# Four state sums at a time in TensorE's column groups, and the D and skip terms as diagonal matmuls, in a selective-scan stage

## The chip, the cores and the metric

The kernel runs on one NeuronCore of a Trainium2 chip. The metric is the device time of one execution in microseconds (us); the median over several runs is compared. The engines are TensorE (PE in the profile; PEld is its weight load), VectorE (DVE), ScalarE (ACT), GpSimd (POOL) and the DMA-issuing SyncE (SP). Each takes its instructions in the order in which the program issues them, and engines wait for each other by semaphores.

## The reference

The program is a convolution, state-space and attention hybrid, followed by an attention layer and a routed mixture of experts, on x of shape (4, 256, 32, 32). The part that matters here is the state-space block. The 256 channels are split in NB = 4 groups of 64; each group of each of the 4 images passes through:

```python
def selective_scan(u, dt, Bm, Cm, A, Dp):
    dA = jnp.exp(dt[..., None] * A)
    dBu = (dt * u)[..., None] * Bm[:, :, None, :]
    def step(h, inp):
        dA_t, dBu_t, C_t = inp
        h = dA_t * h + dBu_t
        return (h, jnp.einsum('bds,bs->bd', h, C_t))
    ...
    return ys.transpose(1, 0, 2) + u * Dp
...
    y = selective_scan(u, dt, Bm, Cm, -jnp.exp(alog), dp)
    return y * jax.nn.silu(z) @ outw.T
...
xm = mamba_v(xc, ...) + skip_scale * xc
```

There are 128 inner channels d, 16 states s and 1024 time steps. So each of the 16 pairs of group and image needs 128 x 16 recurrences over 1024 steps, then the sum over states of h times C, the term u * D, the gate silu(z), the output projection, and the skip term.

## The kernel before, in words

A tile of 128 partitions holds 8 channels times 16 states, with time along the free dimension. So a pair (the profile's blocks of 16 steps, n = 0 to 15) takes 16 tiles, j = 0 to 15, and the stage has 256 steps t = 16 n + j. The main loop of the stage (L808 to L837) is written out by hand, and nothing reorders it. In step t it issues:

- on VectorE, dBu times B (L813), in place in PSUM, then the scan (L816), which writes the tile hs;
- on GpSimd, hs times C (L817);
- on VectorE and GpSimd, when j = 2, `gated` of the pair before: u times D plus pY (L479), then times the gate sz (L480);
- on TensorE, `select(t + 2)` (L770): two bf16 matmuls that spread the rows of dt * u that belong to tile t + 2 over the states. Its PSUM tile dBu has two buffers, so it waits for scan t;
- on TensorE, `add_up(t - 2)` (L778): two fp32 matmuls of 128x128 by 128x512 that add hs over the states into pY. The weight is a window in a 0/1 strip that puts the 8 sums on the 8 right rows of pY and zeros elsewhere, accumulated over the 16 tiles;
- on SP, `fetch(t + 4)` (L758), the broadcast load of dt for a tile (dA, five buffers), and on ScalarE `decay(t + 3)` (L763), the exponential of it;
- the steps of `front` for the next pair (L388 to L464): four projections at j = 11 to 14 (L400), Silu at 15, then the dt projection at 0 (L411), ScalarE functions at 1, `rest` at 3 (L422, VectorE), `log` at 4 (L425, and on GpSimd L426), `dt_out` at 5 (L429), `times_u` at 6 (L434), the bf16 parts at 8 and 10 (L438 to L444), `spread` of B and C at 8 and 9 (L457, L459), and the transfers of `turn` at 11 (L449, L452);
- for the pair before, `project_out` at j = 6 (L487) and, on VectorE, `store` at j = 7 (L493): the skip scale times xm plus the projection, in place; and at j = 10 `gate` of the present pair (L472, L474).

All the large projections share one PSUM tile, mm. The tile hs comes from the pool `scan` with four buffers; the scan of step t overwrites the hs of step t - 4, which L778 must have read.

```python
hs = hss[t] = sp.tile([P, N], F32, tag="hs", name="hs")
nc.vector.tensor_tensor_scan(hs, dAs.pop(t), dBu, 0.0, ALU.mult, ALU.add)
nc.gpsimd.tensor_tensor(hs, hs, r["C"], ALU.mult)
if j == 2 and n > 0:
    gated(n - 1)
select(t + 2)
add_up(t - 2)
fetch(t + 4)
decay(t + 3)
```

Ahead of this loop a short planned stage normalises x and makes the first pair's inputs; the images' x tiles lie in the hs buffers (two images) and in the pool `lnA`. Behind it come the convolutions, two attentions and the experts, which the diff doesn't touch.

Of the kernel before, what the change touches and what calls it, by code (L numbers as in the profile page):

```python
# [10 lines left out]
F32 = mybir.dt.float32  # L11
BF16 = mybir.dt.bfloat16
AF = mybir.ActivationFunctionType
ALU = mybir.AluOpType
# [4 lines left out]
N = HH * WW  # L19
NP = N + 2  # L20
P = 128
# [295 lines left out]
def body(tc, g, out):  # L317
# [5 lines left out]
    def pool(name, bufs, **kw):  # L323
        return tc.tile_pool(name=name, bufs=bufs, **kw)

    with pool("const", 1) as cp, pool("dram", 1, space=bass.MemoryType.DRAM) as drp, contextlib.ExitStack() as late:
# [16 lines left out]
        def V(name, j=0, n=1):  # L343
            return vec[:, VOFF[name] + j : VOFF[name] + j + n]
# [28 lines left out]
        with pool("mconst", 1) as mc, pool("front", 1) as fp, pool("dts", 2, space=bass.MemoryType.DRAM) as dsp, pool(  # L373
# [5 lines left out]
            aneg = mc.tile([P, NB * DS], F32, tag="aneg", name="aneg")  # L379

            def block(nb, b):
                q0 = (nb % 2) * DM
                return slice(q0, q0 + DM), XM[b][q0 : q0 + DM, nb // 2]
# [4 lines left out]
            def front(n):  # L388
# [32 lines left out]
                def rest():  # L421
                    stt(r["e"], r["pdt"], -1.0, r["e"], ALU.add, ALU.subtract)  # L422

                def log():
                    act(r["pdt"], r["pdt"], AF.Ln)  # L425
                    nc.gpsimd.tensor_tensor(r["dt"], r["dt"], r["e"], ALU.subtract)  # L426

# [48 lines left out]
            def gated(n):  # L476
                nb, b = order[n]
                u = state[n]["u"]
                stt(u, u, V("dd", nb), state[n]["pY"], ALU.mult, ALU.add)  # L479
                nc.gpsimd.tensor_tensor(u, u, state[n]["sz"], ALU.mult)  # L480

            def project_out(n):
                nb, b = order[n]
                rows_out, xb = block(nb, b)
                po = state[n]["po"] = big()
                for h in HALVES:
                    mm(po[rows_out, h], m_out[:, nb, :], state[n]["u"][:, h], start=True, stop=True)  # L487

            def store(n):
                nb, b = order[n]  # L490
                rows_out, xb = block(nb, b)
                xb = xb[:, XL : XL + N]
                stt(xb, xb, V("skip")[rows_out], state[n]["po"][rows_out], ALU.mult, ALU.add)  # L493

            state = {}
            with pool("scan", 4) as sp, pool("yps", 1, space=PSUM) as yps, pool("dps", 2, space=PSUM) as dps, pool("lnA", 1) as wp:

# [7 lines left out]
                add, pre.spare, pre.slack, pre.split = pre.add, (2, 3), 700, True  # L505
                xs = [[sp.tile([P, N], F32, tag="hs", name="hs") for k in range(CT)] for b in range(2)]
                for b in range(2, B):
                    t = wp.tile([P, CT, N], F32, tag=f"xs{b}", name=f"xs{b}")
                    xs.append([t[:, k] for k in range(CT)])
# [8 lines left out]
                m_dt = load("m_dt", [DTR, NB, DIN], where=mc)  # L518
                pickf = wp.tile([96, 32 // DB, P], F32, tag="pickf", name="pickf")
                nc.sync.dma_start(out=pickf, in_=g["pick"].rearrange("k (j p) -> k j p", j=32 // DB))  # L520
# [157 lines left out]
                def weights():  # L678
# [74 lines left out]
                dAs, dBus, hss = {}, {}, {}  # L753

                def fetch(t):
                    if t < NBLK:
                        dAs[t] = sp.tile([P, N], F32, tag="dA", name="dA", bufs=5)
                        nc.sync.dma_start(out=dAs[t], in_=state[t // NJ]["ds"][t % NJ].unsqueeze(0).to_broadcast([DS, DB, N]))  # L758

                def decay(t):  # L760
                    if t < NBLK:
                        c = order[t // NJ][0] * NJ + t % NJ
                        act(dAs[t], dAs[t], AF.Exp, scale=aneg[:, c : c + 1])  # L763

                def select(t):
                    if t < NBLK:
                        j = t % NJ
                        dBus[t] = dps.tile([P, N], F32, tag="dBu", name="dBu")
                        for h in HALVES:
                            mm(dBus[t][:, h], pick[:, j % 4], state[t // NJ]["U"][:, j // 4, h], start=True, stop=True)  # L770

                def add_up(t):
                    if 0 <= t < NBLK:
                        r, j, hs = state[t // NJ], t % NJ, hss.pop(t)
                        if j == 0:
                            r["pY"] = yps.tile([P, N], F32, tag="y", name="pY")
                        for h in HALVES:
                            mm(r["pY"][:, h], strip[:, P - DB - j * DB : 2 * P - DB - j * DB], hs[:, h], start=j == 0, stop=j == NJ - 1)  # L778

# [1087 lines left out]
```

## Time and profile before

| what | us |
| --- | --- |
| time, median of 3 runs (lowest, highest) | 3326.42 (3322.93, 3326.98) |
| the profiled execution's own time | 3332.46 |
| its span, first to last instruction | 3330.7 |
| stage of the scans, first L813 to last scan's end | 103.06 to 1197.82 = 1094.8 |
| busy in that stage: VectorE, TensorE, GpSimd, ScalarE | 958.0, 890.5, 775.5, 573.9 |
| granted TensorE clock in that stage, share of full | 0.93 |

A line of the timeline gives the start, the busy time, the engine, the source line, the operation, output and inputs, the shapes, and in brackets the idle time before it with the instruction whose end released it. Matmul ends are modelled; starts are better than ends for telling how long TensorE was occupied. A group line of the page gives the total busy time, the mean ns of one, then the idle time before such instructions and what ended most of it.

### The profile page before, as it was taken

Reading aid. Unit: us, or ns where it says so; the run is one execution under the profiler, and the core shown is the slowest. Engines: PE = TensorE matmul, PEld = TensorE weight load, DVE = VectorE, ACT = ScalarE, POOL = GpSimd, SP = SyncE. Lnnn points to the kernel's source line nnn. Section 1 sums busy time; section 2 is a strip of 40 time slices with the busy share of each in tenths; the row PEclk is TensorE's granted clock in tenths of the full one; section 3 lists DMA queues with packets and bytes.
Section 4 is the critical chain, followed back from the end, with each engine's and each line's share of the span. In section 5 each row is a group of like instructions: output and inputs, shape, how many; then the busy total and the mean of one; then the engine's idle time right before and its main releaser. Section 6 shows DMA issues by size and latency. Waiting matters only on the chain. (4 is left out here: it accounts for less than half of the span.)

```text
span 3330.7 us, 38748 instructions
## 1 busy us (share of the span) xinstructions
PE 2907.4 (87%) x15274; PEld 1693.4 (51%) x15274; DVE 2077.2 (62%) x2347; ACT 1513.0 (45%) x2086; POOL 1223.0 (37%) x763
## 2 busy tenths in 40 slices
PE   7787788878888668998889989989899999899997
PEld 4333333333333224555555554655555656689996
DVE  5789888888888954746496478557364445511112
ACT  3646445554455423545673574565443333311111
POOL 0677767667767730000000010000002222556662
PEclk7899999998999988999999989999999999999998
DMA  3566555656557630000000000000000000465455
GB/s 125 133 159 160 152 145 149 167 145 156 143 150 170 153 113 0 1 1 1 26 1 1 26 1 1 1 14 1 1 13 7 13 7 14 117 193 131 117 124 157
DMA packets 92872, 265.50 MB, mean 80 GB/s; under 512 B 18182, under 2 KB 36086, under 8 KB 89360
## 3 DMA queue, kind: packets, MB, share of 16 engines
q1 hardware_dynamic: 64000, 198.46, 22.7%
q0 software_dynamic: 26512, 60.35, 7.1%
q10 hardware_dynamic: 2176, 4.19, 0.3%
q8 instruction: 121, 1.98, 0.2%
q14 instruction: 63, 0.52, 0.1%
HBM read 291.70 MB, written 42.80 MB: 100 GB/s over the span
## 5 line engine op out<-in xcount | busy, mean ns | idle before, releaser
L817 POOL TENSOR_TENSOR hs<-hs,bc 128x1024 f32<-128x1024 f32 x256 | 602.1, 2357 | 277.1 <-DVE hs L816 276.9
L816 DVE TENSOR_TENSOR_SCAN hs<-dA,dBu 128x1024 f32<-128x1024 f32 x256 | 585.4, 2287 | 73.8 <-PE pY L778 44.0
L778 PE MATMUL pY<-hs,const 128*128 128x512 f32 x1024 | 530.1, 643 | 15.6 <-DVE u L479 12.8
L763 ACT ACTIVATE dA<-dA,aneg 128x1024 f32<-128x1024 f32 x256 | 287.4, 1144 | 331.6 <-DMA dA<-ds 331.1
L1082 DVE TENSOR_REDUCE nm<-s 128x1 f32<-128x1024 f32 x256 | 301.6, 1219 | 203.4 <-PE s L1077 202.7
L1087 ACT ACTIVATE pr<-s,nm 128x1024 f32<-128x1024 f32 x256 | 284.9, 1116 | 196.9 <-DVE nm L1082 194.7
L1101 PE MATMUL k<-const,pr 128*128 128x128 f32 x2048 | 301.1, 291 | 72.8 <-ACT pr L1087 49.1
L1172 POOL TENSOR_TENSOR b<-b,misc 128x1024 f32<-128x1024 f32 x16 | 36.4, 2299 | 893.3 <-DVE misc L1168 835.0
L1101 PEld LDWEIGHTS k<-const,pr 128*128 128x128 f32 x2048 | 234.1, 147 | 191.8 <-issue 82.4
L770 PE MATMUL dBu<-U,pick 96*128 96x512 bf16 x512 | 162.7, 401 | 186.3 <-DVE hs L816 182.4
L813 DVE TENSOR_TENSOR dBu<-dBu,bc 128x1024 f32<-128x1024 f32 x256 | 311.8, 1218 | 4.0 <-PE dBu L770 3.9
L778 PEld LDWEIGHTS pY<-hs,const 128*128 128x128 f32 x1024 | 208.4, 205 | 204.4 <-issue 165.6
L1077 PE MATMUL s<-b,b 32*128 32x512 f32 x1024 | 286.9, 648 | 3.3 <-ACT pr L1087 3.3
L1107 ACT COPY pT<-k 128x512 f32<-128x512 f32 x320 | 175.8, 593 | 173.0 <-PE k L1101 171.8
L1742 PE MATMUL s<-pT,b 128*128 128x128 f32 x1920 | 230.0, 276 | 3.4 <-DMA b<-we,intse 2.9
L1742 PEld LDWEIGHTS s<-pT,b 128*128 128x128 f32 x1920 | 226.1, 192 | 8.6 <-ACT pT L1745 4.0
L770 PEld LDWEIGHTS <-pick 96*128 96x128 bf16 x512 | 41.8, 99 | 370.3 <-issue 303.6
L1107 DVE COPY pT<-k 128x512 f32<-128x512 f32 x192 | 131.6, 686 | 99.7 <-PE k L1101 85.4
L1746 DVE TENSOR_TENSOR pT<-pT,s 128x512 f32<-128x512 f32 x72 | 49.4, 687 | 228.2 <-ACT pT L1745 228.1
L1121 PE MATMUL k<-pT,b 128*32 128x128 f32 x4096 | 152.2, 290 | 17.9 <-DVE pT L1107 14.8
L1121 PEld LDWEIGHTS k<-pT,b 128*32 128x32 f32 x4096 | 113.1, 115 | 74.4 <-issue 31.1
L1077 PEld LDWEIGHTS s<-b,b 32*128 32x128 f32 x1024 | 102.4, 190 | 91.8 <-issue 76.5
(434 smaller groups left out, 4430.4 us busy)
## 6 DMA issues: line engine op xcount, KB each, us to landing
dA<-ds SPq DMA_DIRECT2D x256, 512.0 KB, 4.8
dq<-parts SPq DMA_DIRECT2D x15, 768.0 KB, 3.3
U<-dq SPq DMA_DIRECT2D x45, 256.0 KB, 4.1
ds<-dt SPq DMA_DIRECT2D x16, 512.0 KB, 3.0
b<-x SPq DMA_DIRECT2D x4, 1024.0 KB, 7.2
acc<-pr SPq DMA_DIRECT2D x8, 512.0 KB, 5.8
xm<-x SPq DMA_DIRECT2D x4, 1024.0 KB, 5.0
tokens<-pr SPq DMA_DIRECT2D x8, 512.0 KB, 2.9
```

What stands on the lines that cost most here:

```text
L763: act(dAs[t], dAs[t], AF.Exp, scale=aneg[:, c : c + 1])
L778: mm(r["pY"][:, h], strip[:, P - DB - j * DB : 2 * P - DB - j * DB], hs[:, h], start=j == 0, stop=j == NJ - 1)
L813: tt(dBu, dBu, r["B"], ALU.mult)
L816: nc.vector.tensor_tensor_scan(hs, dAs.pop(t), dBu, 0.0, ALU.mult, ALU.add)
L817: nc.gpsimd.tensor_tensor(hs, hs, r["C"], ALU.mult)
L1077: mm(S[i][:, HALVES[h]], qT[rr, qt * P : (qt + 1) * P], kT[rr, HALVES[h]], start=True, stop=True)
L1082: "DVE", 1220, lambda i=i, u=u: nc.vector.tensor_reduce(nms[u], S[i], AX.X, ALU.max, negate=True),
L1087: "ACT", 1330, lambda i=i, u=u, hd=hd: act(prs[u % 4], S[i], AF.Exp, bias=nms[u], scale=1.0, accum_out=rss[b % 2][:, k, qt, hd : hd + 1]), ...
L1101: nc.tensor.transpose(bank.t[:, j * P : (j + 1) * P], prs[u][:, c0 : c0 + P], ident)
L1107: lambda dst=dst, bank=bank, on_act=on_act: (nc.scalar.copy if on_act else nc.vector.tensor_copy)(dst, bank.t),
L1121: mm(bank.t[i * HD : (i + 1) * HD, 0:P], v[:, 4 * jh + j, hd * HD : (hd + 1) * HD], pTs[m][jh][:, i, j * P : (j + 1) * P], start=j == 0, s ...
L1742: mm(p12[:, a, c], wbufs[w][:, o : o + P], xT[:, k], start=k == 0, stop=k == CT - 1)
```

## The change

- `add_up` does nothing in three steps of four. In the fourth it adds four hs tiles at once: eight fp32 matmuls with 32-column weights, tile i to rows 32 i to 32 i + 31 of pY, for each half of the columns. To make this fit, step t now takes tile `which(t)` of its pair (0, 4, 8, 12, 1, 5, ...), in `fetch`, `decay` and `select` alike.
- With the second group of a pair, two full matmuls with diag(D) add u * D into pY. `gated` becomes one VectorE product of pY and sz; its GpSimd product is gone.
- `project_out` first multiplies xm by diag(skip) into the same PSUM rows, two more matmuls; `store` becomes a copy on ScalarE.
- The GpSimd subtraction of `log` (j = 4) moves to `rest` (j = 3).
- The pool `scan` gets six buffers for hs; the x tiles of a third image move into them, and pickf into the sz tile. Five diagonal matrices are made at the start.

```diff
+            ddiag = mc.tile([P, NB, P], F32, tag="ddiag", name="ddiag")
+            sdiag = mc.tile([P, P], F32, tag="sdiag", name="sdiag")
...
                 def rest():
                     stt(r["e"], r["pdt"], -1.0, r["e"], ALU.add, ALU.subtract)
+                    nc.gpsimd.tensor_tensor(r["dt"], r["dt"], r["e"], ALU.subtract)
 
                 def log():
                     act(r["pdt"], r["pdt"], AF.Ln)
-                    nc.gpsimd.tensor_tensor(r["dt"], r["dt"], r["e"], ALU.subtract)
...
             def gated(n):
-                nb, b = order[n]
-                u = state[n]["u"]
-                stt(u, u, V("dd", nb), state[n]["pY"], ALU.mult, ALU.add)
-                nc.gpsimd.tensor_tensor(u, u, state[n]["sz"], ALU.mult)
+                tt(state[n]["u"], state[n]["pY"], state[n]["sz"], ALU.mult)
...
                 for h in HALVES:
-                    mm(po[rows_out, h], m_out[:, nb, :], state[n]["u"][:, h], start=True, stop=True)
+                    mm(po[rows_out, h], sdiag[rows_out, rows_out], xb[:, XL + h.start : XL + h.stop], start=True, stop=False)
+                    mm(po[rows_out, h], m_out[:, nb, :], state[n]["u"][:, h], start=False, stop=True)
...
-                xb = xb[:, XL : XL + N]
-                stt(xb, xb, V("skip")[rows_out], state[n]["po"][rows_out], ALU.mult, ALU.add)
+                nc.scalar.copy(xb[:, XL : XL + N], state[n]["po"][rows_out])
...
-            with pool("scan", 4) as sp, ...
+            with pool("scan", 6) as sp, ...
...
-                xs = [[sp.tile([P, N], F32, tag="hs", name="hs") for k in range(CT)] for b in range(2)]
-                for b in range(2, B):
+                xs = [[sp.tile([P, N], F32, tag="hs", name="hs") for k in range(CT)] for b in range(B - 1)]
+                for b in range(B - 1, B):
...
+                    for nb in range(NB):
+                        add("DVE", 150, lambda nb=nb: ts(ddiag[:, nb], ident, V("dd", nb), None, ALU.mult))
+                    add("DVE", 150, lambda: ts(sdiag, ident, V("skip"), None, ALU.mult))
...
+                def which(t):
+                    return t % 4 * 4 + t % NJ // 4
...
                 def add_up(t):
-                    if 0 <= t < NBLK:
-                        r, j, hs = state[t // NJ], t % NJ, hss.pop(t)
-                        if j == 0:
+                    if 0 <= t < NBLK and t % 4 == 3:
+                        r, q = state[t // NJ], t % NJ // 4
+                        four = [hss.pop(t - 3 + i) for i in range(4)]
+                        if q == 0:
                             r["pY"] = yps.tile([P, N], F32, tag="y", name="pY")
                         for h in HALVES:
-                            mm(r["pY"][:, h], strip[:, P - DB - j * DB : 2 * P - DB - j * DB], hs[:, h], start=j == 0, stop=j == NJ - 1)
+                            for i in range(4):
+                                mm(
+                                    r["pY"][32 * i : 32 * i + 32, h], strip[:, P - DB - q * DB : P - q * DB + 32 - DB], four[i][:, h],
+                                    start=q == 0, stop=q == 3,
+                                )
+                        if q == 1:
+                            for h in HALVES:
+                                mm(r["pY"][:, h], ddiag[:, order[t // NJ][0]], r["u"][:, h], start=False, stop=False)
```

More of the change, by code (lines that the diff above doesn't have):

```diff
@@ L491, in store @@
                 rows_out, xb = block(nb, b)
-                xb = xb[:, XL : XL + N]
-                stt(xb, xb, V("skip")[rows_out], state[n]["po"][rows_out], ALU.mult, ALU.add)
+                nc.scalar.copy(xb[:, XL : XL + N], state[n]["po"][rows_out])
             state = {}
-            with pool("scan", 4) as sp, pool("yps", 1, space=PSUM) as yps, pool("dps", 2, space=PSUM) as dps, pool("lnA", 1) as wp:
+            with pool("scan", 6) as sp, pool("yps", 1, space=PSUM) as yps, pool("dps", 2, space=PSUM) as dps, pool("lnA", 1) as wp:
                 pre = Plan()
@@ L518, in body @@
                 m_dt = load("m_dt", [DTR, NB, DIN], where=mc)
-                pickf = wp.tile([96, 32 // DB, P], F32, tag="pickf", name="pickf")
+                pickf = fp.tile([P, N], F32, tag="sz", name="sz")[:96, : 32 // DB * P].rearrange("k (j p) -> k j p", p=P)
                 nc.sync.dma_start(out=pickf, in_=g["pick"].rearrange("k (j p) -> k j p", j=32 // DB))
@@ L757, in fetch @@
                         dAs[t] = sp.tile([P, N], F32, tag="dA", name="dA", bufs=5)
-                        nc.sync.dma_start(out=dAs[t], in_=state[t // NJ]["ds"][t % NJ].unsqueeze(0).to_broadcast([DS, DB, N]))
+                        nc.sync.dma_start(out=dAs[t], in_=state[t // NJ]["ds"][which(t)].unsqueeze(0).to_broadcast([DS, DB, N]))
                 def decay(t):
                     if t < NBLK:
-                        c = order[t // NJ][0] * NJ + t % NJ
+                        c = order[t // NJ][0] * NJ + which(t)
                         act(dAs[t], dAs[t], AF.Exp, scale=aneg[:, c : c + 1])
@@ L766, in select @@
                     if t < NBLK:
-                        j = t % NJ
+                        j = which(t)
                         dBus[t] = dps.tile([P, N], F32, tag="dBu", name="dBu")
```

## The prediction

> **What bounds the kernel now.** I read the page first, then the engine timelines inside the scan stage, then the granted clock. The page gives totals over stages with different limits, so it only says where to look.
>
> ```profile
> PE 2907.4 (87%) x15274; PEld 1693.4 (51%) x15274; DVE 2077.2 (62%) x2347; ACT 1513.0 (45%) x2086; POOL 1223.0 (37%) x763
> L816 DVE TENSOR_TENSOR_SCAN hs<-dA,dBu 128x1024 f32<-128x1024 f32 x256 | 585.4, 2287 | 73.8 <-PE pY L778 44.0
> L778 PE MATMUL pY<-hs,const 128*128 128x512 f32 x1024 | 530.1, 643 | 15.6 <-DVE u L479 12.8
> ```
>
> The change touches only the stage with the 256 scans: 103.06 to 1197.82 us, 1094.8 of the span's 3330.7. In it VectorE is busy 958.0 us and TensorE 890.5, so VectorE leads and each of its waits is lost time. Its timeline shows three kinds of step:
>
> ```profile
> 506.79 1.23 DVE L813 TENSOR_TENSOR dBu<-dBu,bc 128x1024 f32<-128x1024 f32 x1
> 508.68 2.29 DVE L816 TENSOR_TENSOR_SCAN hs<-dA,dBu 128x1024 f32<-128x1024 f32 x1 [0.65 <-PE pY L778]
> ...
> 531.22 1.28 DVE L479 SCALAR_TENSOR_TENSOR u<-u,vec,pY 128x1024 f32<-128x1024 f32 x1
> 532.41 1.22 DVE L813 TENSOR_TENSOR dBu<-dBu,bc 128x1024 f32<-128x1024 f32 x1
> ...
> 545.50 1.22 DVE L429 TENSOR_TENSOR dt<-dt,mm 128x1024 f32<-128x1024 f32 x1 [0.87 <-POOL dt L426]
> 546.64 1.23 DVE L813 TENSOR_TENSOR dBu<-dBu,bc 128x1024 f32<-128x1024 f32 x1
> ...
> 556.16 1.29 DVE L493 SCALAR_TENSOR_TENSOR xm<-xm,vec,mm 64x1024 f32<-64x1024 f32 x1 [2.40 <-PE mm L487]
> 557.47 1.23 DVE L813 TENSOR_TENSOR dBu<-dBu,bc 128x1024 f32<-128x1024 f32 x1
> ...
> 561.01 1.21 DVE L813 TENSOR_TENSOR dBu<-dBu,bc 128x1024 f32<-128x1024 f32 x1
> 562.34 2.29 DVE L816 TENSOR_TENSOR_SCAN hs<-dA,dBu 128x1024 f32<-128x1024 f32 x1
> 564.55 1.21 DVE L813 TENSOR_TENSOR dBu<-dBu,bc 128x1024 f32<-128x1024 f32 x1
> ```
>
> A free step is 564.55 - 561.01 = 3.54 us. A step in which a scan waits for L778 loses 0.65 (its hs buffer is still read by the sum). Four extra VectorE operations per block of 16 steps cost, start to next start, 1.19 (L479), 1.12 (L422), 1.14 (L429) and 1.31 (L493); L429 waits 0.87 for GpSimd, L493 2.40 for the projection. Blocks 1 to 14 (scan starts 176.39 to 1139.17) take 68.77 us each: 16 x 3.54 = 56.64, 4.76 of extras, about 7.4 of waits. Block 15 has nothing beside it: 56.35 from its first scan to its last. Now TensorE:
>
> ```profile
> 506.59 1.88 PE L778 MATMUL pY<-hs,const 128*128 128x512 f32 x4
> 508.40 1.98 PE L400 MATMUL mm<-xm,m_cu 64*128 64x512 f32 x4
> ...
> 541.51 3.28 PE L778 MATMUL pY<-hs,const 128*128 128x512 f32 x4
> ...
> 1607.95 1.08 PE L1121 MATMUL k<-pT,b 128*32 128x128 f32 x32
> 1608.97 0.66 PE L1101 MATMUL k<-const,pr 128*128 128x128 f32 x4
> ```
>
> Each fp32 matmul is two records of 0.43 us at 512 columns, so a step's sum is 4 x 0.43 = 1.72; at 541.51 the same four take 3.28. The granted clock explains it; in this view the columns are stretch, length, PE busy, clock, DMA share, GB/s:
>
> ```profile
> 537.50:540.92 3.42, 1.05 (x4) 1.00 0.47 143
> 540.92:544.33 3.41, 3.41 (x6) 0.50 0.65 150
> 544.33:547.74 3.41, 2.66 (x7) 1.00 0.08 24
> ```
>
> The clock changes on a grid of 3.41 us: after a stretch only 31% busy it is halved, after a fully busy one it is back. That matters more below than any instruction count.
>
> **The change, part by part.** *Column groups (L778).* Sixteen sums per block of 1.72 each become four bursts of eight 32-column matmuls. Whether four run at once is bounded by L1121, which has 32-column weights, 128 rows and four different moving tiles: 32 records of 128 columns (0.107 each in turn, 3.4 us) go from 1607.95 to 1608.97, 1.02 us. So at best a burst is 4 x 0.43 = 1.72 plus about 0.1 (1.02 less 8 x 0.107, halved) for each change of form; at worst, one after the other, 16 x 0.43 = 6.9. I take 1.72, the nearest row. TensorE's load falls by about 20 us per block, and the 0.65 waits and the 2.40 go.
>
> *The new wait.* Six hs buffers against four, but all four of a group are held until its burst. Scan 4q+6 overwrites hs of 4q, which the burst reads; the burst stands in step 4q+5, on TensorE behind the selection of step 4q+7, and that waits for scan 4q+5, whose dBu bank it takes. So once per four steps there is a chain from the end T of a scan to the next scan: 0.14 until the selection starts (540.65 to 540.79), 0.43 for it (536.11 to 536.54), 0.1 form change, 1.72 burst, 0.37 until the scan (506.59 + 1.72 to 508.68) = 2.76. VectorE would be ready at T + 1.33 (561.01 to 562.34). Stall 1.43 at full clock. At half clock: 0.14 + 0.86 + 0.1 + 3.4 + 0.6 = 5.1, stall 3.8, less what the clock's return inside the run gives back (0 to 1). Behind the waiting scan stand all of VectorE, then GpSimd's product and the next dBu bank.
>
> *Which clock.* Step numbers j in a block: bursts at j = 1, 5, 9, 13. In j = 2 to 4 TensorE has only the selection, 0.43 of 3.54 to 4.7 us, about 10% busy; by the 31% row the clock is halved at j = 5. There L429 (1.14) covers part: 3.8 - 1.14 = 2.7, with some return 2.5. In j = 15 it is the same, so j = 0 (selection 0.86, dt projection 3.4 at half clock, over 3.54) runs late into the burst at j = 1, during which the clock returns: 2.9 (bounds 1.43 and 3.8). From j = 6 the projection with the new skip matmuls (4 x 0.86 + form changes) keeps it busy, so j = 9 is mostly full clock: 1.6. At j = 13 it is at full clock, but the projection (1.92 per step, behind gate's Silu) delays the selection by some 0.3: 1.7. Sum 8.7; bounds 1.43 + 0.3 + 1.43 + 1.7 = 4.9 and 3.8 + 2.7 + 3.4 + 3.4 = 13.3.
>
> *VectorE.* L493 goes (1.31). L479 becomes a plain product, priced as L429, 1.14. The subtraction on GpSimd, one step earlier, ends before L429 needs it, and the 0.87 goes. Per block 56.64 + 1.14 + 1.12 + 1.14 = 60.04.
>
> *Added elsewhere.* ScalarE: a 64x1024 copy, about 1.0 (L459's 1012 ns), hidden: ScalarE is busy 574 of 1095 us. It stands ahead of decay 11, which is due three steps later (over 10 us); cover gone, it would cost that 1.0 per block. GpSimd loses one product, 2.36. D term: two matmuls, 1.72, behind the burst at j = 9, hidden since the next selection is due 5 us later. Five 128x128 diagonals on VectorE at the start, by the nearest row (L693, 128x64, 0.18 at 12.74 us) near 0.2 each, stand right ahead of the first reduction at 13.79: 0 if x lands later, 1 us otherwise; I take 1. SP keeps its queue order; the fetches read other rows of the same size.
>
> **The sum.** Blocks 1 to 14: 60.04 + 8.7 = 68.74 against 68.77, nothing. Block 15: no fronts, four cold bursts near 3 us: 15 x 3.54 + 1.14 + 12 = 66.2 against 56.35, +10. Block 0: three bursts (2.5 + 1.6 + 1.7) and 2.26 of extras against 4.9 now: +3. After the last scan: the cold burst and the skip matmuls add about 2.4, GpSimd's 2.34 goes: 0. Start: +1. Total +14. The profiled execution took 3332.46 us (span 3330.7); it would become 3346. The median lies 6.0 lower, so 3326.4 + 14 = 3340.
>
> Against this, the Trainium skill, "TensorE: Matmul & The Clock Gate", Part 1, ties the drop to an idle window of about 3.4 us and puts the ramp at under 1% of a span for modelling. The 31% row contradicts it: that stretch held work and the clock fell. By the page the gaps of some 3.1 us would leave the clock full, which is the first rival below. The same page, Part 3, measures 3.07x for four row tiles and 2.38x for three column tiles; L1121 shows 3.3x. By the page's 3.07 a burst would take some 0.4 more, 25 us over 63 bursts.
>
> **The rivals.** *The clock stays full* (faster). For: the bursts and projections together fill over half of TensorE's time. Against: the 31% row, and steps with only a selection. Stalls 4.9: (64.94 - 68.77) x 14 = -54; block 15 with 4 x 1.43: 53.1 + 1.14 + 5.7 = 59.9, +3.6; block 0: -0.4; start +1. 3276. It can't go much further, since decay of step 16 now ends 1.2 us before its scan (518.83 + 1.15 against 521.17), behind the U transfers.
> *The bursts at j = 9 and 13 are cold too* (slower). For: TensorE's load halves, and it returns only after a nearly full window. Against: the projections of j = 10 to 14 fill 2.35 of 3.54. Sum 2.9 + 2.5 + 3.4 + 3.4 = 12.2: (72.24 - 68.77) x 14 + 14 = +63, 3389. It decides from two lost windows per block.
> *The groups don't run four at once at 512 columns* (the change does not do what it says). For: no row shows 512. Against: L1121. Two at a time: each burst 1.72 longer, at half clock 3.4: near 6.5 per block, +110, 3436.
>
> **How the numbers follow.** Break-even in the middle with losses at the ends: 0.52, own range 3310 to 3365. Full clock 0.24; cold bursts 0.15; no four at once 0.09. Range 3270 to 3400: it leaves out about half of the first rival's lower side (0.1), the last (0.09) and a little of the second. A difference of 0.2% (6.6 us) is about what a measurement of this kernel can tell. Faster: 0.24 + 0.08 of the likeliest = 0.32; same 0.15; slower 0.53.
>
> **What would show it.** Right: scans at j = 2, 6, 10, 14 wait for the sums' matmuls, 63 times, some 2.1 us each, and no other scan does; clock 0.5 in j = 2 to 5; burst records in fours within 0.43. Wrong: no such waits (then the buffers are freed otherwise and the time nears 60 per block, below the range), or bursts of 3.4 us at clock 1.0. Blocks of 65 us mean the clock stayed up.

## The result, and the profile after

The changed kernel takes 3437.72 us (median of 4 runs, 3436.47 to 3438.59) against 3324.68 us for the kernel before (4 runs): a ratio of 1.0341, 95% interval 1.0323 to 1.0359. The change makes the kernel slower by 113 us.

The page of the changed kernel, with the lines that answer to those of before: busy times, the granted clock in 40 slices, and the groups of the scan and of the sums.

```profile
PE 2843.1 (83%) x15402; PEld 1557.5 (45%) x15402; DVE 2048.5 (60%) x2336; ACT 1531.7 (45%) x2102; POOL 1184.4 (34%) x747
...
PEclk8666666766666666899999999999999999999998
...
L832 DVE TENSOR_TENSOR_SCAN hs<-dA,dBu 128x1024 f32<-128x1024 f32 x256 | 585.3, 2286 | 225.7 <-PE pY L788 202.2
...
L788 PE MATMUL pY<-hs,const 128*32 128x512 f32 x1024 | 183.3, 838 | 5.5 <-POOL hs L833 5.5
```

Every engine but ScalarE has less to do than before, and the sums fall from 530.1 to 183.3 us. Yet the scans' waits for them rise from 44.0 to 202.2 us, and the clock's digits are 6 and 7 in nearly every slice of the scan stage (0.67 on average there, 0.93 before). VectorE's waits, in the view that sorts them by what was waited for (us in total, times, longest):

```profile
DVE hs L832 <- PE pY L788: 202.2, 63, 7.2
...
DVE dBu L829 <- PE dBu L777: 45.5, 22, 2.6
```

There are 63 of the first kind, as the prediction counted, but 3.2 us each and not 2.1. The second kind, products that wait for the selection, took 3.9 us in all before.

Where the time went, from the starts of the scans (L816 before, L832 after). The spans grew by 3434.7 - 3330.7 = 104.0; the profiled execution of before was some 8 us above the median of all its runs, which accounts for most of the difference from 113.

| us | before | after | grew by | predicted |
| --- | --- | --- | --- | --- |
| start to first scan | 104.40 | 97.33 | -7.1 | +1 |
| block 0 | 71.99 | 82.28 | +10.3 | +3 |
| blocks 1 to 14, each | 68.77 | 74.90 | 14 x 6.13 = +85.8 | 0 |
| block 15, first to last scan | 56.35 | 70.82 | +14.5 | +10 |
| last scan to the end | 2135.2 | 2135.7 | +0.5 | 0 |
| sum | | | +104.0 | +14 |

So the loss lies in the repeated block. There, the time from one scan's start to the next, less the 3.54 of a free step, is zero but for these steps (means of blocks 1 to 14): 1.13 at j = 2, 1.10 at j = 3 and 1.14 of j = 5 are the three operations that VectorE keeps, as predicted. The rest is waiting: 1.93 behind j = 1, 2.29 behind j = 5, 2.69 behind j = 8, 1.45 behind j = 9 and 6.56 behind j = 13, in sum 14.9 where the prediction had 8.7. VectorE's timeline in block 5 (start, busy, line, shapes, idle before) shows the last four:

```profile
509.10 2.29 DVE L832 TENSOR_TENSOR_SCAN hs<-dA,dBu 128x1024 f32<-128x1024 f32 x1 [2.43 <-PE pY L788]
...
520.97 1.23 DVE L829 TENSOR_TENSOR dBu<-dBu,bc 128x1024 f32<-128x1024 f32 x1 [2.55 <-PE dBu L777]
...
527.29 2.29 DVE L832 TENSOR_TENSOR_SCAN hs<-dA,dBu 128x1024 f32<-128x1024 f32 x1 [1.58 <-PE pY L788]
...
540.94 1.23 DVE L829 TENSOR_TENSOR dBu<-dBu,bc 128x1024 f32<-128x1024 f32 x1 [0.74 <-PE dBu L777]
548.85 2.29 DVE L832 TENSOR_TENSOR_SCAN hs<-dA,dBu 128x1024 f32<-128x1024 f32 x1 [6.68 <-PE pY L788]
```

And TensorE's timeline in the same stretch:

```profile
505.44 3.64 PE L788 MATMUL pY<-hs,const 128*32 128x512 f32 x16
511.44 1.01 PE L777 MATMUL dBu<-U,pick 96*128 96x512 bf16 x2 [2.36 <-DVE hs L832]
512.38 1.97 PE L487 MATMUL mm<-xm,sdiag 64*64 64x512 f32 x2
514.28 1.97 PE L488 MATMUL mm<-u,m_out 128*64 128x512 f32 x2
...
518.07 1.97 PE L488 MATMUL mm<-u,m_out 128*64 128x512 f32 x2
519.97 1.39 PE L777 MATMUL dBu<-U,pick 96*128 96x512 bf16 x4
...
525.18 1.92 PE L788 MATMUL pY<-hs,const 128*32 128x512 f32 x16
...
536.15 3.78 PE L403 MATMUL mm<-xm,m_cu 64*128 64x512 f32 x4 [1.79 <-ACT sz L477]
539.87 1.03 PE L777 MATMUL dBu<-U,pick 96*128 96x512 bf16 x2
540.83 3.77 PE L403 MATMUL mm<-xm,m_cu 64*128 64x512 f32 x4
544.54 1.04 PE L777 MATMUL dBu<-U,pick 96*128 96x512 bf16 x2
545.50 3.15 PE L788 MATMUL pY<-hs,const 128*32 128x512 f32 x16
```

The groups do run four at once at 512 columns: 16 records in 1.92 us at full clock (525.18), 3.64 at half. Behind j = 8, the selection at 519.97 stands behind eight half-clock matmuls of skip and output projection, 512.38 to 519.97. Behind j = 13, the burst at 545.50 stands behind two projections that take 3.78 each, where they take 1.98 at full clock, and itself takes 3.15. TensorE isn't short of time here; it is at half clock at the wrong moments. The granted clock in stretches of its own grid (stretch, length, PE busy, clock, DMA share, GB/s):

```profile
513.89:517.31 3.42, 3.42 (x5) 0.50 0.58 96
517.31:520.72 3.41, 3.41 (x5) 0.50 0.76 225
530.97:534.38 3.41, 2.72 (x7) 1.00 0.60 147
534.38:537.79 3.41, 1.64 (x2) 0.50 0.28 117
537.79:541.20 3.41, 3.41 (x6) 0.50 0.47 158
541.20:544.62 3.42, 3.42 (x5) 0.50 1.09 234
544.62:548.03 3.41, 3.41 (x14) 0.50 1.03 221
548.03:551.44 3.41, 2.79 (x14) 1.00 0.87 192
```

This is not the rule that the prediction read from before. There one fully busy stretch brought the clock back. Here it stays at half after fully busy stretches (513.89, 537.79 and 541.20, filled mostly by matmuls of 64 rows or 64 columns) and comes back after others (517.31, 544.62), and it falls at 534.38 after a stretch that was 80% busy (530.97: gate matmuls with 64 rows, bf16 selections with 96). What tells these stretches apart is worked out behind the experiments.

### The profile page after: what moved, and what is told of

It is laid out like the page before. It is cut to its first block, busy times and chain, and to the rows that moved or that the text cites. A ratio compares the mean times of both kernels' runs of the same rounds, so it can differ in the third digit from the quotient of the medians.

```text
span 3434.7 us, 38975 instructions
## 1 busy us (share of the span) xinstructions
PE 2843.1 (83%) x15402; PEld 1557.5 (45%) x15402; DVE 2048.5 (60%) x2336; ACT 1531.7 (45%) x2102; POOL 1184.4 (34%) x747
## 5 line engine op out<-in xcount | busy, mean ns | idle before, releaser
L832 DVE TENSOR_TENSOR_SCAN hs<-dA,dBu 128x1024 f32<-128x1024 f32 x256 | 585.3, 2286 | 225.7 <-PE pY L788 202.2
L777 PE MATMUL dBu<-U,pick 96*128 96x512 bf16 x512 | 215.5, 521 | 337.7 <-DVE hs L832 336.9
L788 PE MATMUL pY<-hs,const 128*32 128x512 f32 x1024 | 183.3, 838 | 5.5 <-POOL hs L833 5.5
L403 PE MATMUL mm<-xm,m_cu 64*128 64x512 f32 x240 | 162.4, 810 | 25.1 <-ACT sz L477 25.1
```

## The experiments

The kernel before ran beside each group of runs, at 3324.68 us for the changed kernel, 3326.39 for the next four rows of the table, 3338.96 for the four behind them and 3343.81 for the last four, so ratios are compared. The columns with j are the mean distance of scan starts in blocks 1 to 14, behind step j, less 3.54; j = 2 holds 1.13 of VectorE's own work and j = 5 holds 1.04 to 1.14. There is no column for j = 0, where the time is under 0.6 but for fill everywhere (1.18), pairs with Silu early (1.29) and pairs with turn on GpSimd (1.16).

| kernel | ratio to before [95%] | block | j=1 | j=2 | j=5 | j=8 | j=9 | j=13 | j=14 | j=15 |
| --- | --- | --- | --- | --- | --- | --- | --- | --- | --- | --- |
| changed | 1.0341 [1.0323, 1.0359] | 74.90 | 1.93 | 1.13 | 3.43 | 2.69 | 1.45 | 6.56 | 0 | 0 |
| eight buffers | 0.9879 [0.9860, 0.9897] | 65.78 | 0 | 1.84 | 1.04 | 0 | 0 | 1.87 | 1.05 | 2.39 |
| burst first | 1.0125 [1.0108, 1.0142] | 71.30 | 1.97 | 1.13 | 1.10 | 2.76 | 0.51 | 6.02 | 0 | 0.07 |
| fill everywhere | 1.0280 [1.0255, 1.0305] | 73.85 | 3.25 | 1.13 | 2.85 | 4.44 | 1.45 | 1.83 | 0 | 0 |
| no groups | 0.9836 [0.9814, 0.9859] | 65.58 | 0 | 2.08 | 1.04 | 0.67 | 0.36 | 0.56 | 0.61 | 0.77 |
| fill late | 1.0243 [1.0216, 1.0271] | 73.18 | 5.43 | 1.13 | 3.19 | 2.48 | 1.45 | 1.79 | 0 | 0 |
| eight and fill late | 0.9889 [0.9863, 0.9915] | 65.87 | 0 | 4.60 | 1.04 | 0 | 0 | 0 | 0.23 | 1.67 |
| pairs | 0.9804 [0.9778, 0.9830] | 64.00 | 0.08 | 4.37 | 1.04 | 0.42 | 0 | 0 | 0.03 | 0.36 |
| full rows | 1.0248 [1.0222, 1.0275] | 72.99 | 3.73 | 1.13 | 3.19 | 2.50 | 1.45 | 3.22 | 0 | 0 |
| no skip matmuls | 1.0391 [1.0369, 1.0413] | 76.48 | 1.96 | 1.13 | 3.43 | 0 | 2.37 | 7.35 | 0 | 0 |
| fill late, Silu early | 1.0121 [1.0095, 1.0147] | 70.58 | 2.07 | 1.13 | 3.12 | 2.31 | 1.45 | 2.45 | 0 | 0 |
| pairs, Silu early | 0.9711 [0.9684, 0.9738] | 62.13 | 0 | 1.54 | 1.04 | 0.18 | 0 | 0 | 0.03 | 0.40 |
| pairs, turn on GpSimd | 1.0001 [0.9986, 1.0015] | 68.48 | 0.17 | 1.58 | 1.04 | 0.51 | 0 | 0 | 0.03 | 6.33 |

### Eight buffers for hs

```diff
-            with pool("scan", 6) as sp, ...
+            with pool("scan", 8) as sp, ...
...
-                for b in range(B - 1, B):
-                    t = wp.tile([P, CT, N], F32, tag=f"xs{b}", name=f"xs{b}")
-                    xs.append([t[:, k] for k in range(CT)])
+                xs.append([fp.tile([P, N], F32, tag="sz", name="sz"), fp.tile([P, N], F32, tag="u", name="u", bufs=3)])
```

The space comes from laying the fourth image's x tiles elsewhere; four small set-up steps move two or four scan steps earlier for it.

> Eight hs buffers in place of six (the fourth image's x tiles lie in sz and u, pickf in dt). The blocks of the changed kernel lose 2.0, 2.3, 2.7, 1.45 and 6.7 us at j = 2, 6, 9, 10 and 14, all but the third as a scan that waits for a burst. Theory buffers (a scan is tied to a burst that stands late on TensorE): those four waits go, 12.5 us per block, and what is left is the selection's wait near j = 9: blocks of 62 to 64 us, total near 3240. Theory clock (TensorE at half rate is late with everything, selections too): the waits move from the scans to the dBu products, blocks stay at 70 or more, total 3360 or above.

Measured: 3284.49 us (3281.42 to 3290.66). All the waits of scans for sums are gone, behind j = 1, 5, 9 and 13 alike, so it was the tie through the six buffers that held the scans. What is left is the clock's part: products wait for selections that stand behind half-clock projections, in all

```profile
DVE dBu L827 <- PE dBu L775: 80.3, 45, 3.6
```

and the clock falls and stays down in the same steps. The stretches of this kernel at such a place:

```profile
551.33:554.75 3.42, 2.49 (x6) 0.90 0.00 0
...
558.16:561.57 3.41, 3.41 (x6) 0.50 0.48 117
561.57:564.99 3.42, 3.42 (x9) 0.50 1.07 218
```

These stretches lie 0.7 us behind the clock's grid. The first is 73% busy (gate matmuls and a selection) and the clock drops near its end, hence the 0.90; the other two are filled mostly by 64-row projections, and it doesn't come back in them. Neither theory had the whole: the buffers are worth 1.0341 - 0.9879, 4.6% of the time before, and the clock keeps some 5 us per block (j = 13 to 15).

### The burst ahead of the selection

```diff
-                        select(t + 2)
                         add_up(t - 2)
+                        select(t + 2)
```

> The burst is issued ahead of the selection in its step, still six buffers. Theory order (the burst is late because the selection ahead of it waits for the scan before): the burst starts when GpSimd has its fourth product, some 2 us or more ahead of that scan's end, and the waits at j = 2, 6 and 10 fall below 0.5 each, the one at j = 14 to 3 or 4: total 3437 - 16 x 8 = near 3310. Theory depth (six buffers are too few wherever the burst stands): waits stay, total above 3400. Theory clock: the bursts still take 3.4 at half clock; the gain is the 0.9 of a cold selection per burst, total near 3380.

Measured: 3369.17 us (3366.28 to 3370.67), between the theories. Without the selection ahead of it the burst doesn't wait for the running scan, and the waits behind j = 5 (2.29 to none) and j = 9 (1.45 to 0.51) go. Those behind j = 1 and 13 stay: there the burst stands behind cold projections, not behind the selection. The order is a part of the chain, as the prediction had it, in two of four places.

### Filling TensorE's idle time

The selection is repeated in steps where TensorE has little to do; the repeats write the same values. First in seven of 16 steps:

```diff
-                        select(t + 2)
+                        select(t + 2, {2: 5, 3: 5, 4: 5, 7: 5, 15: 5, 10: 3, 11: 3}.get(j, 1))
```

> The selection is issued five times over in steps j = 2, 3, 4, 7, 15 and three times in 10 and 11 (the same result written again), so that TensorE isn't idle there; nothing else differs. Theory clock: the granted clock in the stage rises from some 0.65 to over 0.9, the waits shrink to the full-clock sizes (1.4, 0.3, 0, 1.4, 1.7), blocks of 65 us, total near 3285, although TensorE does more work. Theory buffers and order alone: the clock may rise but the waits stay near 10 per block, total above 3380; if the extra work only makes TensorE late, above 3437.

Measured: 3423.46 us (3411.10 to 3424.61). The wait behind j = 13 falls from 6.56 to 1.83 (1.70 in most blocks, with the clock at 1.00 there), which is just what the prediction had put for it at full clock. But the extra work itself made the burst at j = 1 and the selection at j = 8 late, and the sum hardly moved. The stage's clock rose to 0.79 only, not over 0.9, and the 3285 that came with it was missed. So only the two steps ahead of j = 13 were filled:

```diff
+                        select(t + 2, {10: 3, 11: 3}.get(j, 1))
```

> The changed kernel (six buffers) with the selection issued three times over at j = 10 and 11 alone. Theory clock: TensorE's idle microseconds around gate's Silu halve the clock and make it late for the burst at j = 13; with the clock kept, the scan wait there falls from 6.5 or 7.4 to 1.7 per block and all other waits stay: total 3437 - 14 x 5 = near 3367. Theory buffers and order alone: the clock is a bystander, total stays above 3420.

Measured: 3418.41 us (3414.24 to 3422.09). Again j = 13 gives up 4.8 us, and j = 1 takes 3.5 of them, though nothing near it was touched, so the 3367 expected was missed by far. The timelines of ScalarE, TensorE and VectorE in this kernel show the next limit:

```profile
537.36 1.15 ACT L770 ACTIVATE dA<-dA,aneg 128x1024 f32<-128x1024 f32 x1 [8.87 <-DMA dA<-ds]
...
544.29 1.11 ACT L407 ACTIVATE u<-mm,vec 128x1024 f32<-128x1024 f32 x1
...
545.46 3.43 PE L414 MATMUL mm<-u,m_wdt 128*128 128x512 f32 x4 [2.94 <-ACT u L407]
...
549.26 1.92 PE L788 MATMUL pY<-hs,const 128*32 128x512 f32 x16
...
551.37 2.29 DVE L832 TENSOR_TENSOR_SCAN hs<-dA,dBu 128x1024 f32<-128x1024 f32 x1 [5.27 <-PE pY L788]
```

The Silu behind the projections (L407) stands on ScalarE behind decays that wait for their fetches; the dt projection (L414) waits for the Silu, the burst stands behind it on TensorE, and the scan waits for the burst. In the changed kernel the long wait behind j = 13 had given the fetches time: there this Silu starts some 3 us behind the start of scan j = 15 in most blocks, here some 1 us behind that of scan j = 1, two scans later.

### Eight buffers and the late fill

Both edits together.

> Eight hs buffers and the selection three times over at j = 10 and 11. With eight buffers the blocks still lose 1 to 2.6, 1.1 and 2 to 2.8 us at j = 13 to 15, as dBu products that wait for selections behind half-clock projections. Theory buffers and clock together: these go too, blocks of 61 to 63 us, total 3284 - 14 x 4.5 = near 3220. If the projections are late at full clock as well: no change, 3275 or more.

Measured: 3300.48 us (3297.77 to 3303.33), the same ratio as with eight buffers alone and not the 3220 expected. The waits behind j = 13 and 14 go and that behind j = 15 shrinks; j = 2 takes as much, through the late Silu: the gated product waits for pY.

### Projections with 128 rows

Is it the 64 rows that leave the clock down? The four projections are widened to 128 rows; the added rows have zero weights, so the sums and the number of columns stay as they were. This kernel lays the x tiles out as the one with eight buffers does, but keeps six.

```diff
-                        mm(r["pu"][:, h], m_cu[rows_in, nb // 2, k], xb[:, k + h.start : k + h.stop], ...)
+                        mm(r["pu"][:, h], m_cu[:, nb, k], XM[b][:, nb // 2, k + h.start : k + h.stop], ...)
```

> The changed kernel (six buffers, x of the fourth image moved as in the eight-buffer kernel) with the four projections of a block widened from 64 to 128 rows by zero weights: the same matmuls, the same time each, no more idle cover. Theory (the clock counts how much of the array works, and 64-row matmuls count as half): the projections keep or regain the clock at j = 12 and 13, the wait at the burst of j = 13 falls from some 6.6 to 2 or 3, total near 3375. Rival (only the time busy counts): the clock falls there as before, total 3425 to 3440.

Measured: 3420.87 us (3412.18 to 3422.13). The mean clock in step 13 rises from 0.52 to 0.80 and the wait behind it falls from 6.56 to 3.22, with not one matmul more. The total is not the theory's 3375, for the time shows up behind j = 1 again (3.73), as in the late fill. The stretches of the clock's grid in block 5:

```profile
518.33:521.74 3.41, 1.62 (x5) 1.00 0.15 63
521.74:525.15 3.41, 3.41 (x6) 0.50 0.49 178
525.15:528.57 3.42, 3.42 (x21) 1.00 1.04 238
```

The clock still falls, behind a stretch in which TensorE waits for gate's Silu. But one stretch full of 128-row projections and a selection brings it back, where two with 64 rows (537.79 and 541.20 in the changed kernel) didn't. In blocks 1 to 13 the half clock lasts one such stretch in nine blocks and two in four; in the changed kernel it lasts three or four.

### The change without its groups

All the other parts of the change, six buffers among them, but full-width sums in every step, with tiles in their old order and the D term at j = 5.

```diff
                 def which(t):
-                    return t % 4 * 4 + t % NJ // 4
+                    return t % NJ
...
+                            mm(r["pY"][:, h], strip[:, P - DB - j * DB : 2 * P - DB - j * DB], hs[:, h], start=j == 0, stop=j == NJ - 1)
```

> Everything of the change but the column groups: full-width sums in every step as in the kernel before, six buffers, D and skip on TensorE, copy on ScalarE, earlier subtraction. Theory groups (the loss is all from bursts and the idle, half-clock TensorE that they leave): no scan waits in bursts, clock back over 0.9, blocks of 62 to 66 us, total 3230 to 3300, under the kernel before. Rival, the skip and D matmuls or the copy on ScalarE cost the time: total stays above 3380.

Measured: 3269.48 us (3267.43 to 3279.54). The full-width sums keep the clock at 0.90 or above in every step, and nothing waits long. So the other parts bring 1.6% and the groups of four, with six buffers, cost 1.0341 - 0.9836 = 5.1%.

### Groups of two

Two tiles at a time, 64 columns each: the sums take twice the time that groups of four take, but a burst holds only two hs, and it comes every second step.

```diff
-                    return t % 4 * 4 + t % NJ // 4
+                    return t % 2 * 8 + t % NJ // 2
...
-                                    r["pY"][32 * i : 32 * i + 32, h], strip[:, P - DB - q * DB : P - q * DB + 32 - DB], four[i][:, h],
+                                    r["pY"][64 * i : 64 * i + 64, h], strip[:, P - DB - q * DB : P - q * DB + 64 - DB], four[i][:, h],
```

> Two hs tiles at a time in 64-column groups in place of four in 32-column ones, six buffers: a burst of four matmuls every second step, whose hs are overwritten six steps on, so no scan stands close behind a burst, and TensorE is less idle. Theory buffers: no scan waits for bursts, blocks of 61 to 64 us, total near 3240, under the kernel before. Theory clock: select-only steps still halve the clock and the selections come late near j = 9 and 13: blocks near 67, total near 3310.

Measured: 3271.91 us (3264.49 to 3274.99). No scan waits for sums any more, with six buffers. The one long wait left is behind j = 2, 4.37 less 1.13. Timelines of ScalarE, TensorE and VectorE:

```profile
485.51 1.15 ACT L770 ACTIVATE dA<-dA,aneg 128x1024 f32<-128x1024 f32 x1 [8.04 <-DMA dA<-ds]
...
492.55 1.11 ACT L407 ACTIVATE u<-mm,vec 128x1024 f32<-128x1024 f32 x1
...
493.71 3.78 PE L414 MATMUL mm<-u,m_wdt 128*128 128x512 f32 x4 [4.02 <-ACT u L407]
...
498.27 1.94 PE L788 MATMUL pY<-hs,const 128*64 128x512 f32 x8
...
500.28 1.22 DVE L480 TENSOR_TENSOR u<-pY,sz 128x1024 f32<-128x1024 f32 x1 [4.16 <-PE pY L788]
```

It is the chain of the late fill: decay, Silu, dt projection, last sums, and here the gated product.

### The skip term back on VectorE

```diff
-                    mm(po[rows_out, h], sdiag[rows_out, rows_out], ...)
-                    mm(po[rows_out, h], m_out[:, nb, :], state[n]["u"][:, h], start=False, stop=True)
+                    mm(po[rows_out, h], m_out[:, nb, :], state[n]["u"][:, h], start=True, stop=True)
...
-                nc.scalar.copy(xb[:, XL : XL + N], state[n]["po"][rows_out])
+                stt(xb, xb, V("skip")[rows_out], state[n]["po"][rows_out], ALU.mult, ALU.add)
```

> The changed kernel with the skip term back on VectorE (no skip matmuls, no storing copy on ScalarE). Theory: the 2.7 us before scan j = 8 are the selection for j = 8 standing behind eight half-clock 64-row matmuls of skip and output projection (7.9 us in a row); with four of them (3.9 us) the selection is on time and that wait goes. But VectorE takes its 1.24 us operation back and waits in it for the output projection, some 3 to 4 us as it did before the change (3.7 us each). Blocks 1 to 13 then stay at 75 to 77 us, total 3430 to 3470. Rival (the skip matmuls are to blame for the cold clock and the waits at large): blocks fall below 73, total below 3410.

Measured: 3471.44 us (3468.48 to 3475.77). The wait behind j = 8 is gone, and 2.52 us appear behind j = 7. Timelines of TensorE and VectorE:

```profile
519.36 3.68 PE L487 MATMUL mm<-u,m_out 128*64 128x512 f32 x4
...
523.08 1.27 DVE L493 SCALAR_TENSOR_TENSOR xm<-xm,vec,mm 64x1024 f32<-64x1024 f32 x1 [1.19 <-PE mm L487]
```

So the 2.69 did come from the skip matmuls at half clock, and the operation that they replace costs 2.52 in nearly the same place. Behind j = 9 and 13 another 0.9 and 0.8 appear, and blocks come to 76.48, within what the theory had. Leaving the skip matmuls out wins nothing.

### The Silu ahead of the decay

If the late Silu is the next limit, it can be issued earlier: the last part of the projections goes to j = 13 and the Silu to j = 14, ahead of that step's decay.

```diff
-                return [(i - 5, lambda i=i: project(i)) for i in range(4)] + [
-                    (-1, silu), (0, project_dt), ...
+                return [(min(i - 5, -3), lambda i=i: project(i)) for i in range(4)] + [
+                    (-2, silu), (0, project_dt), ...
```

With the late fill:

> The changed kernel with the selection three times at j = 10 and 11 (as in the run that filled TensorE late), and the conv projections' last part at j = 13 and the Silu at j = 14, ahead of that step's decay, so that it isn't behind decays that wait for late transfers. Theory: the rise at j = 1 in the run without the second edit (2.0 to 4.7-6.0 us) was the burst standing behind the dt projection that waited for this Silu; with the Silu some 3 us earlier the wait at j = 1 goes back to 2 to 3 us, the one at j = 13 stays at 1.7, blocks are 69 to 71, ratio to the kernel before 1.00 to 1.015. Rival (the rise is the scans being ahead of what the transfers can supply, whatever ScalarE's order): the time shows up at another step, as decays waiting for transfers, and blocks stay at 72 to 74, ratio 1.02 to 1.03.

Measured: 3383.12 us (3375.30 to 3388.03). The wait behind j = 1 goes from 5.43 to 2.07, and the ratio is 1.0121, within what was expected. The wait behind j = 13 stays at 1.7 in 11 of the 14 blocks, but two have 6 us there.

With the groups of two:

> Sums over two tiles at a time (as in the run of pairs), and the Silu at j = 14 ahead of that step's decay. Theory: what was left there, 3 to 5.7 us at j = 2, is the gated product waiting for pY, whose last sums stand behind a dt projection that waits for the Silu; with the Silu some 3 us earlier 2 to 3 us of it go in each of 14 blocks: blocks of 59 to 63 us, total 30 to 45 us below the run of pairs, ratio 0.965 to 0.975. Rival (transfers set the pace there): the waiting moves to scans that wait for decays, ratio stays at 0.978 to 0.983.

Measured: 3248.89 us (3237.78 to 3260.96). It beats both kernels: 2.9% less than the kernel before [2.6%, 3.2%], 6% less than the changed one by the ratios. Timelines of ScalarE, TensorE and VectorE, at the place shown for the groups of two:

```profile
485.01 1.11 ACT L407 ACTIVATE u<-mm,vec 128x1024 f32<-128x1024 f32 x1
...
486.57 1.88 PE L414 MATMUL mm<-u,m_wdt 128*128 128x512 f32 x4
...
491.55 1.94 PE L788 MATMUL pY<-hs,const 128*64 128x512 f32 x8
...
494.42 1.20 DVE L480 TENSOR_TENSOR u<-pY,sz 128x1024 f32<-128x1024 f32 x1
```

Nothing here waits for the Silu now. Of the 3.2 us, 2.8 went behind j = 2; 1.29 came behind j = 0, where scans now wait for decays.

### The transfers of `turn` on GpSimd's queue

The decays' fetches stand on SP behind the four transfers that turn U. In the kernel with groups of two those four are issued by GpSimd in their stead.

```diff
-                    nc.sync.dma_start(out=dq, in_=r["parts"])
+                    nc.gpsimd.dma_start(out=dq, in_=r["parts"])
...
-                        nc.sync.dma_start(out=U[32 * q : 32 * q + 32], ...)
+                        nc.gpsimd.dma_start(out=U[32 * q : 32 * q + 32], ...)
```

> Sums over two tiles at a time, with the four transfers that turn U issued from GpSimd's queue and not SP's, so that the decays' fetches don't stand behind their waits. Theory (the root of the late Silu and so of the j = 2 wait is SP's order): the decays' 8 us wait at the block's end goes, the Silu is on time, the wait at j = 2 falls from 3 to 5.7 us to under 2, ratio 0.96 to 0.975. Rival: GpSimd waits in its own order for the first transfer to land, its products come 2 to 4 us late, the sums with them, and the wait only changes its place: ratio 0.978 or above.

Measured: 3341.22 us (3334.29 to 3349.24), ratio 1.0001. Each theory holds in part: behind j = 2 the time falls from 4.37 to 1.58, but behind j = 15 there are now 6.33 us. Timelines of GpSimd, TensorE, VectorE and ScalarE:

```profile
574.59 1.66 POOL L455 DMA_DIRECT2D U<-dq  x3 [4.72 <-DMA dq<-parts]
...
583.34 1.01 PE L777 MATMUL dBu<-U,pick 96*128 96x512 bf16 x2 [7.38 <-DMA U<-dq]
584.39 1.23 DVE L829 TENSOR_TENSOR dBu<-dBu,bc 128x1024 f32<-128x1024 f32 x1 [6.03 <-PE dBu L777]
...
588.10 1.11 ACT L407 ACTIVATE u<-mm,vec 128x1024 f32<-128x1024 f32 x1 [9.40 <-PE mm L403]
```

GpSimd waits 4.72 us for the first transfer, and the next block's first selection waits for U. The decays of the next block's first three tiles wait 3.4 us in all for their fetches where they waited 10.4 with groups of two (means of blocks 1 to 14), so that wait does come mostly from SP's order. The Silu is not on time for it: it now waits 9.40 us for the last projection, which stands behind that selection. Whether the 2.8 us won behind j = 2 come from SP's order or from the 6.33 us that the scans now lose just before isn't shown.

## Why the prediction was right or wrong, point by point

- **The mechanism is right.** Scans wait for bursts because a group holds four of six hs buffers: 63 waits at the four places named, none with eight buffers, none with groups of two. The order inside the chain (selection ahead of burst) is right for j = 5 and 9, as the run with the burst first shows.
- **Four groups at once is right:** 16 records in 1.92 us, against 1.72 plus about 0.1. The rival that put the kernel at 3436 is refuted, though the time lies there: it was to come from bursts of 3.4 us at full clock, so its number is right by luck. (Its price of 6.5 per block is also less than its own terms: four bursts, each 1.72 longer, are 6.9, and more where they are cold.) The rival with the clock at full is refuted too: the clock is 0.50 in j = 3 to 5.
- **VectorE's terms are right:** 1.13, 1.10 and 1.14 against 1.14, 1.12 and 1.14, and the 0.87 went.
- **The stall at j = 5 is right** (2.29 against 2.5), with the clock at 0.50 there; j = 1 was put at 2.9 and measured 1.93. The number for j = 9 is right (1.45 against 1.6), but in part by luck. The skip matmuls were to keep TensorE busy, and so the clock up, from j = 6 on; the clock was 0.50 in j = 6 and 7 and 0.54 in j = 8, and in block 5 it came back at 520.72, 4.5 us ahead of that burst.
- **The step that failed is "At j = 13 it is at full clock ... 1.7".** The clock there is 0.52 on average, and the stall 6.56, 4.9 us more in the mean of 14 blocks: 68 of the 90 us by which the spans' sum was off. With TensorE filled just before, the clock is full there and the stall is 1.70 in 13 of the 14 blocks: the chain was sized right, its clock wasn't. The clock rule came from stretches of before in which the full 128-row sums ran in every step. With those gone, a stretch 80% busy with 64-row gate matmuls and selections let the clock fall, and fully busy ones with 64-row projections don't bring it back. Nor does the upper bound given for that step, 3.4, hold it: it priced a cold burst, but not the two cold projections ahead of it, 2 x 1.8 us more, and the first of these late by 1.79 behind the gate's Silu. The rival with cold bursts at j = 9 and 13 had the clock of j = 13 right, at that price, and the clock of j = 9 wrong (0.89).
- **A term was missing: j = 8,** 2.69 us, 38 in 14 blocks. It is the same mistake: the skip matmuls were priced as work that keeps TensorE busy and the clock up. At half clock, skip and output projection take 7.6 us in a row and the selection behind them is late. The run without them shows it; it also shows that VectorE's operation in their stead costs as much. What j = 1 gained over its estimate (1.0) and the small differences make up the rest: 68 + 38 - 14 - 6 = 86, the blocks' growth.
- **Blocks 0 and 15** grew by 10.3 and 14.5 against 3 and 10. The wait behind j = 13 is 7.86 in block 0, where 1.7 was put; in block 15 the four bursts cost 3.1 to 3.6 each, near the 3 predicted, and 2.68 behind j = 8 were missing there as well. **The start** gained 7.1 where +1 was put; see the last section.
- **The limit of the fast rival was named rightly.** "It can't go much further", since the decays stand behind the U transfers: with the waits taken out, that chain is what came next, by way of the Silu, and moving the Silu won 1.2% with the late fill and 0.9% with groups of two.
- The Trainium skill, "TensorE: Matmul & The Clock Gate", Part 1, gives the warm-up as about 3.4 us of time, not as a number of matmuls. The runs here don't bear that out where 64-row or 64-column matmuls fill the time: 537.79 to 544.62 is 6.8 us at half clock without a break. The measurement decides.

What the clock follows can be read from all the traces together. The scan stages of the 14 kernels hold 4554 stretches of the 3.41 us grid. Weigh the time of each matmul (up to the start of the next one) by the rows of its weight, as a share of 128, add it up in each stretch, and look at the clock of the stretch behind it:

| clock in the stretch | busy share, weighed by rows | stretches | followed by full clock |
| --- | --- | --- | --- |
| half | under 0.70 | 1072 | 0 |
| half | 0.70 to 0.85 | 351 | 83 |
| half | 0.85 or more | 572 | 572 |
| full | under 0.40 | 557 | 0 |
| full | 0.40 to 0.50 | 247 | 171 |
| full | 0.50 or more | 1755 | 1741 |

The 14 exceptions of the last line are one in each kernel, all between 101 and 115 us, where the scans begin. The plain busy share doesn't sort them: of the stretches at half clock that were 95% busy or more, none of the 178 under 0.70 by rows brought the clock back, and all of the 542 with 0.85 or more did. With one threshold for stretches at half clock, 45 of the 1995 lie on the wrong side by rows, 99 by rows times columns (the groups of a burst taken together), 296 by columns and 394 by plain busy time. The stretches shown fit: 537.79 and 541.20 come to 0.57 and 0.51, 513.89 to 0.78 and 517.31 to 0.83, 544.62 to 0.93, and 530.97, behind which the clock fell, to 0.46; the two that the prediction read in the kernel before come to 0.30 and 0.96. This sorts traces; the kernel with 128-row projections is the one run that changes the rows by themselves. What stays open is whether the number format counts as well, since all matmuls with 96 rows in the loop are bf16.

## What to carry to other kernels

Packing small matmuls into column groups shortens TensorE's work, but it gathers it in bursts that hold every buffer of the group, and it takes away the steady work that kept the clock up; price it with the buffers held until the burst (groups of two were enough here) and with all the neighbouring matmuls at half clock. A clock rule read from a profile holds for the mix of matmuls in that profile: a busy share is not enough when the shapes change, and here it had to be weighed by the matmuls' rows. When a wait is taken out and the time doesn't fall, look for the transfer that the wait had given time, and for what stands behind its consumer in an in-order queue.

## What the runs showed of the hardware that wasn't expected

- At half clock, fully busy stretches of 6.8 us, mostly of 64-row matmuls, left the clock at 0.50 (537.79 to 544.62 in the changed kernel, 558.16 to 564.99 with eight buffers); stretches 80% and 73% busy with such matmuls and selections let it fall (530.97, 551.33).
- Weighed by rows, a busy share of 0.85 or more always brought the clock back and one under 0.70 never did; a share of 0.50 or more kept it, but for one stretch at the start of each scan stage, and one under 0.40 always lost it (the table above).
- Four 32-column groups of 128 rows and 512 columns run at once: 16 records in 1.92 us at full clock (525.18), against 6.9 one after the other.
- The first scan starts at 104.4 us in the kernel before, 97.3 in the changed one, 102.6 with the burst first and 97.6 with the late fill, though the edits of the last two lie in the loop behind that start. So the growth behind the start is 111 us, not 104. The profiled execution of the kernel before was 7.8 us above the median of its runs, so its late start may be that execution's own and no gain of the change; its cause wasn't looked for.
